# Second layer of the mix MLP by Strassen's seven products instead of eight, with GpSimd adds over SBUF and graph loads on SyncE

## The chip, the cores and the metric

The kernel runs on one core of one Trainium2 chip. The metric is the device time of one execution in microseconds (us). The kernel before takes 1915.63 us, the median of three runs (1912.76 to 1917.06).

## What is computed

One layer of a graph transformer over 1250 tokens of 768 features, all in float32, in three parts:

```
xn = layernorm(x)
x  = x + gnn(xn, edges) + mix(xn)         # mix: linear attention, then an MLP
x  = x + ffn(layernorm(x))                # router picks 2 of 4 experts

mix's MLP:  x = x + gelu(h @ fc1_w + fc1_b) @ fc2_w + fc2_b    # 768 -> 3072 -> 768
gnn:        two graph attention layers (4 heads of 192, 2 heads of 96):
            w[s,d] = exp(leaky(a[s] + b[d]) - max) where an edge is; out[d] = sum_s w[s,d] h[s] / sum_s w[s,d]
```

The change touches the second matrix product of mix's MLP (fc2) and the way in which the graph part, which runs beside that MLP, is cut and loaded.

## The kernel before

Tokens lie in 10 tiles of 125 (`TP`). Big matrix products with 768 inputs already use the seven-product scheme of Strassen and Winograd: both operands are cut in two along both sides, some sums of quarters are formed first (`differences` on the token side, L101; `combined` on the weight side, L111), and seven products of quarters take the place of eight. `product` (L123) issues the matmuls of one product; with `more=True` it goes on adding into a bank of PSUM that already holds an earlier product, so that one bank gathers a chain of sums.

The stage in question begins at L953, where the PSUM pools are dealt anew: two banks for the graph part and transposes (`p_tp`), one for a chained bank of fc1 (`p_a`), two for its other products (`p_dc`) and three for all else (`p_m3`). The hidden 3072 features are taken in 12 groups of 256 (`GROUPS`). Each group has two token units (`MIX`, 250 and 375 token pairs). For each unit `fc1_unit` (L967) makes the hidden values in seven steps, chained, with ScalarE copying the chained bank aside between its products (L982, L992, L995) and VectorE adding (L985, L998, L1005), and the gelus on ScalarE (L965). Then fc2 is applied plainly: `fc2_half` (L1009) makes one tile's half of 384 output columns by two matmuls (the two blocks of 128 hidden features, L1016) and VectorE adds the bank into the running sum `xn` in SBUF (L1021). That is 12 groups x 10 tiles x 2 halves = 240 such halves, 480 matmuls; the hardware issues each float32 matmul as two instructions, so the profile counts 960.

The graph part is a generator (`gnn`, L1177). It first finds the largest score of each target (`largest`, L1058: VectorE passes of 1250 columns, L1086, with the adjacency loaded chunk by chunk over GpSimd's queue, L1067). Then, for three groups of target tiles (`SPLITS`: 4, 3 and 3 tiles), for each head and each of ten source chunks, `weighted` (L1128) makes the edge weights: two exponentials on ScalarE (L1144, L1147), a maximum and a minimum-times-adjacency on VectorE (L1149, L1150); the PE multiplies them with the features (L1194 in layer one, L1233 in layer two). The adjacency, the row `bt` and the features come over GpSimd's DMA queue (L1142, L1133, L1182).

What runs when: a pattern of letters (L1338) deals the seven steps of `fc1_unit` (P) and the halves of the unit before (h) in turn, and each puts PE time on an account (`spend`, L1305). When the account covers the next yield of `gnn`, the graph part moves one step on. A scheduler may then move instructions within each engine's stream; those wrapped in `pin` keep their order. [...] In the last group the tiles are finished one by one (`last_tile`, L1314), so that the expert part can begin.

Of the kernel before, what the change touches and what calls it, by code (L numbers as in the profile page):

```python
# [23 lines left out]
MIX, MIX_TILES = [(0, 250), (250, 375)], [(0, 1, 5, 6), (2, 3, 4, 7, 8, 9)]  # L24
# [8 lines left out]
def tile_gps_layer(ctx, tc, a, out):  # L33
# [77 lines left out]
    def combined(engine, w11, w12, w21, w22, to):  # L111

        s1, s2, s4 = (to[:, i] for i in range(3))
        engine.tensor_tensor(s1, w21, w22, ALU.add)
        engine.tensor_tensor(s2, s1, w11, ALU.subtract)
        engine.tensor_tensor(w21, w11, w21, ALU.subtract)
        engine.tensor_tensor(s4, w12, s2, ALU.subtract)
        return w11, w12, w21, w22, s1, s2, s4
# [35 lines left out]
    at = 0  # L154
# [666 lines left out]
    def load_fc2(g, j):  # L821

        if g < GROUPS:
            c0, w = HALVES[j]
            lasts[g, j] = wpool.tile([128, 2, 384], F32, name="w2", bufs=3)
            nc.sync.dma_start(
                lasts[g, j], rows(fc2[g * 256 : (g + 1) * 256, c0 : c0 + w], 128)
            )
# [5 lines left out]
    with tc.tile_pool(name="qp", bufs=1) as qp:  # L834
        wp = weights(qp, "wp", a["L0_mix_proj_w"])
        load_fc1(0)
        load_fc2(0, 0)
        load_fc2(0, 1)
        load_fc1(1)
        load_fc2(1, 0)  # L840
# [114 lines left out]
    p_dc = banks.enter_context(tc.tile_pool(name="p_dc", bufs=2, space=PSUM))  # L955
    p_mm[0] = banks.enter_context(tc.tile_pool(name="p_m3", bufs=3, space=PSUM))
# [10 lines left out]
    def fc1_unit(g, c):  # L967


        c0, w = MIX[c]  # L970
        cs = slice(c0, c0 + w)
        va, vb = (v_of[c][:, i] for i in range(2))
        x11, x21 = fT[:, 0:3, cs], fT[:, 3:6, cs]
        x22, t3 = fT[:, 3:6, HALF + c0 : HALF + c0 + w], x12[:, :, cs]
        t1, t2, t4 = (xt[:, i, :, cs] for i in range(3))
        w11, w12 = list(quarters_of(firsts[g]))[:2] if c == 0 and g else firsts[g][:2]
        pa = p_a.tile([128, 512], F32, name="ps_a")[:, :w]
        pd, pc = (p_dc.tile([128, 512], F32, name=n, tag="dc")[:, :w] for n in ("ps_d", "ps_c"))
        c1 = u3 = hpool.tile([128, 375], F32, name="c1")[:, :w]
        u2 = hpool.tile([128, 375], F32, name="u2")[:, :w]  # L980
        product(nc.tensor, pa, w11, x11)
        nc.scalar.copy(c1, pa)  # L982
        yield
        product(nc.tensor, pd, w12, x21)
        nc.vector.tensor_tensor(va[:, 0, :], pd, c1, ALU.add)  # L985
        gelu(va[:, 0, :], va[:, 0, :], 2 * g)
        if c == 0 and g:
            fc1_sums(g)
        yield
        _, _, s3, w22, s1, s2, s4 = firsts[g]  # L990
        product(nc.tensor, pa, s2, t2, more=True)
        nc.scalar.copy(u2, pa)  # L992
        yield
        product(nc.tensor, pa, s3, t3, more=True)
        nc.scalar.copy(u3, pa)  # L995
        yield
        product(nc.tensor, pc, s1, t1)
        nc.vector.tensor_tensor(vb[:, 1, :], pc, u3, ALU.add)  # L998
        gelu(vb[:, 1, :], vb[:, 1, :], 2 * g + 1)
        yield  # L1000
        product(nc.tensor, pa, w22, t4, more=True)
        gelu(vb[:, 0, :], pa, 2 * g + 1)
        yield
        product(nc.tensor, pc, s4, x22, more=True)
        nc.vector.tensor_tensor(va[:, 1, :], pc, u2, ALU.add)  # L1005
        gelu(va[:, 1, :], va[:, 1, :], 2 * g)
        yield

    def fc2_half(g, c, t, j):  # L1009

        h, i = divmod(t, 5)
        at = i * TP - MIX[c][0]
        o0, ow = HALVES[j]
        ps = bank("ps_f2")[:TP, :ow]
        for f in range(2):
            nc.tensor.matmul(  # L1016
                ps, v_of[c][:, f, h, at : at + TP], lasts[g, j][:, f, :],
                start=f == 0, stop=f == 1,
            )
        o = xn[:, t, o0 : o0 + ow]  # L1020
        nc.vector.tensor_tensor(o, ps, o, ALU.add)  # L1021
# [4 lines left out]
    av2 = gp.tile([TP, 2, 192], F32, name="av2")  # L1026
    nc.sync.dma_start(av2[:, 0, :], bcast(a["L0_gnn_a_src2"].rearrange("h c -> (h c)"), TP))
    nc.sync.dma_start(av2[:, 1, :], bcast(a["L0_gnn_a_dst2"].rearrange("h c -> (h c)"), TP))
# [5 lines left out]
    def load_wu2x():  # L1034
        nc.vector.memset(wu2x[96:97], 0.0)
        nc.vector.memset(wu2x[:, :, 768:769], 0.0)
        nc.vector.memset(wu2x[96:97, :, 768:769], 1.0)

        nc.gpsimd.dma_start(wu2x[96:97, 0, :768], brow_d)
        nc.gpsimd.dma_start(wu2x[:96, :, :768], rows(a["L0_gnn_Wu"][D : D + 192, :], 96))  # L1040

    h2 = gp.tile([TP, NT, 2, 97], F32, name="h2")
    nc.vector.memset(h2[:, :, :, 96:97], 1.0)
# [14 lines left out]
    def largest(heads, s, b_d, pace, before=lambda c: None, behind=lambda: None):  # L1058
# [3 lines left out]
        load = [slot_x[:TP, 5000 + i * N : 5000 + (i + 1) * N] for i in range(2)]  # L1062
        load.append(turns[:TP, 0, :N])
# [31 lines left out]
        for h in range(heads):  # L1095
            for u0 in range(0, NT, 4):
                n = min(4, NT - u0)
                ps = bank("ps_mx").rearrange("p (u c) -> p u c", c=128)
                for u in range(n):
                    pin(nc.tensor.transpose(  # L1100
                        ps[:TP, u, :TP], run[:, h, (u0 + u) * TP : (u0 + u + 1) * TP],
                        ident[:TP, :TP],
                    ))
                nc.vector.tensor_reduce(
                    mx[:, h, u0 : u0 + n], ps[:TP, :n, :TP], AX.X, ALU.max
                )
            yield 2.0
        sd = s[:, 1]
# [10 lines left out]
        ps = bank("ps_row")  # L1119
# [6 lines left out]
        yield from rest(4)  # L1126

    def weighted(g, h, heads, b_d, s, sl):  # L1128

        t0, n = SPLITS[g]  # L1130
        d0, w = t0 * TP, n * TP
        bt = gp.tile([128, 2, 500], F32, name="bt", bufs=2)
        nc.gpsimd.dma_start(  # L1133
            bt[:, :, :w],
            bcast(
                b_d.rearrange("(j h t) p -> j h (t p)", j=2, h=heads)[:, h, d0 : d0 + w], 128
            ),
        )
        for c in range(NT):
            adj = slot_x[:TP, c * 500 : c * 500 + w]  # L1140
            if h == 0:
                nc.gpsimd.dma_start(adj, adj_d[c * TP : (c + 1) * TP, d0 : d0 + w])  # L1142
            e = gp.tile([TP, 2, 500], F32, name="ee", bufs=2)
# [4 lines left out]
            wt = gp.tile([TP, 500], F32, name="wt", bufs=3)  # L1148
            nc.vector.tensor_tensor(wt[:, :w], e[:, 0, :w], e[:, 1, :w], ALU.max)  # L1149
            nc.vector.scalar_tensor_tensor(  # L1150
                wt[:, :w], wt[:, :w], 1.0, adj, op0=ALU.min, op1=ALU.mult
            )
            yield c, wt[:, :w]

    def lagging(steps, run, lag=1):
        held = []
        for x in steps:
# [3 lines left out]
            yield 1.7  # L1161
# [3 lines left out]
    def earlier():  # L1165


        at = [slot_x[:TP, 5000 + i * D : 5000 + (i + 1) * D] for i in range(3)]
        for t in range(NT + 2):
            if t < NT:  # L1170
                nc.gpsimd.dma_start(at[t % 3], raw_d[t])
            if t > 1:
                o = xn[:, t - 2, :]
                nc.vector.tensor_tensor(o, o, at[(t - 2) % 3], ALU.add)
            yield

    def gnn():  # L1177
        feats = {}

        def fetch(h):  # L1180
            gh = turns[:TP, h % 2, :].rearrange("p (t f) -> p t f", f=193)
            pin(nc.gpsimd.dma_start(gh, rows(g1_d[h % 4], TP)))  # L1182
            feats[h % 4] = gh

        yield from largest(4, s1, b1_d, 5.0, merged, lambda: fetch(0))
        fetch(1)
        for g, (t0, n) in enumerate(SPLITS):
            for h in range(4):
                gh = feats[h]
                sums = [bank4("ps_o").rearrange("p a b -> p (a b)") for _ in range(2)]  # L1190
# [10 lines left out]
                yield from lagging(weighted(g, h, 4, b1_d, s1, s1l), add)  # L1201
                if g < 2 or h < 2:
                    fetch(h + 2)
                for i in range(n):
# [9 lines left out]
                    if h == 3:  # L1214
                        for j in range(2):
                            pr = gp.tile([TP, 2, 96], F32, name="pr")
# [9 lines left out]
        for g, (t0, n) in enumerate(SPLITS):  # L1226
            o2 = turns[:97, 1, :1000].rearrange("p (h n) -> p h n", n=500)
            w = n * TP
            for h in range(2):
# [9 lines left out]
                yield from lagging(weighted(g, h, 2, b2_d, s2, s2l), add)  # L1239
                nc.scalar.copy(o2[:, h, :w], sums[:97, :w])  # L1240
            for i in range(n):
                for h in range(2):
                    rd = small.tile([TP, 1], F32, name="rd")
                    for c0, cw in ((384, 385), (0, 384)):
                        ps = bank("ps_u2")
# [74 lines left out]
    def halves_of(g, c):  # L1320
        ts = MIX_TILES[c]
        if g < GROUPS - 1:
            return [(g, c, t, j) for j in range(2) for t in ts]
        return [(g, c, t, j) for t in ts for j in range(2)]

    def put_half(g, c, t, j):
        fc2_half(g, c, t, j)
        spend(1.39)
        if g == GROUPS - 1 and j:
            last_tile(t)  # L1330

    todo = []
    for g in range(GROUPS):
        if g:
            load_fc1(g + 1)
            load_fc2(g, 1)
            load_fc2(g + 1, 0)
        for c, pattern in enumerate(("PPhhhhPhhPPhhPPhhhh", "PPhhPhhPPhhPPhh")):  # L1338
            if g == GROUPS - 1 and c:
# [3 lines left out]
                gnn_pool.__exit__(None, None, None)  # L1343
            parts = fc1_unit(g, c)
            for p in pattern:
                if p == "P":
                    next(parts)
                    if g or c:
                        spend(2.04 if c else 1.36)
                elif todo:  # L1350
                    put_half(*todo.pop(0))
            todo = halves_of(g, c)
    for x in todo:
        put_half(*x)
# [445 lines left out]
```

## Time and profile before

| what | value |
| --- | --- |
| median of three runs | 1915.63 us |
| the profiled execution's own time | 1917.79 us |
| its span, first to last instruction | 1915.7 us |
| PE busy over the span | 1872.7 us, 98% |
| VectorE (DVE), ScalarE (ACT), GpSimd (POOL) busy | 1355.5, 802.8, 502.7 us |
| the MLP stage with the graph part | 552 to 1355 us of the span |
| fc2's matmul instructions (L1016) | 960, from 558 to 1349 us |

A busy time is the union of an engine's instructions; a matmul's end is modelled and reaches over the start of the next, so the mean duration of a matmul is longer than the distance at which they follow each other. In the groups of instructions each row has the source line, the engine, the operation, what it writes and reads, the shape, the count, the busy time, the mean duration in ns, and the idle time of the engine just before. "PEld" is the load of a matmul's stationary operand, which lies beside the matmuls.

### The profile page before, as it was taken

To read this page: it belongs to the slowest core of one execution; us is meant where nothing else is said; L and a number is where in the kernel's file an instruction comes from. 1 tells how busy PE (TensorE), PEld (TensorE's weight loads), DVE (VectorE), ACT (ScalarE), POOL (GpSimd) and SP (SyncE) were. 2 spreads that over 40 slices of the span, in tenths; PEclk is the share of its full clock that TensorE was granted. 3 is DMA by queue.
4 is the path that set the end of the run, shared out by engine and by line. 5 is a ranking of instruction groups with operands and counts; after the bars stand their busy time and mean duration, and the time that the engine had idled before them with its cause. 6 is when DMAs were issued, how large, how long until landed. Compare 5 with 4: busy or idle time off the path is not lost.

```text
span 1915.7 us, 19523 instructions
## 1 busy us (share of the span) xinstructions
PE 1872.7 (98%) x6966; PEld 1244.2 (65%) x6966; DVE 1355.5 (71%) x2372; ACT 802.8 (42%) x1206; POOL 502.7 (26%) x341
## 2 busy tenths in 40 slices
PE   8999899999999999999999999999999999999998
PEld 7555456775556667787877655566766666666664
DVE  4889651379545986676766977865787777777778
ACT  3223231232321117777775166754473343533330
POOL 2167588777851110020210111100131000000000
PEclk9999999999999999999999999999999999999999
DMA  9957711423149742242432542301485201011023
GB/s 342 274 133 177 200 1 2 116 18 66 2 34 158 142 111 76 70 118 74 113 100 56 149 121 82 92 9 52 130 95 90 76 1 66 1 66 38 20 85 110
DMA packets 184284, 175.49 MB, mean 92 GB/s; under 512 B 110043, under 2 KB 153595, under 8 KB 182908
## 3 DMA queue, kind: packets, MB, share of 16 engines
q0 software_dynamic: 126640, 68.01, 20.7%
q1 hardware_dynamic: 54270, 98.48, 16.3%
q10 hardware_dynamic: 3278, 7.75, 1.3%
q8 instruction: 55, 0.90, 0.2%
q14 instruction: 41, 0.34, 0.1%
HBM read 137.80 MB, written 42.05 MB: 94 GB/s over the span
## 4 chain that ended last, share of the span: by engine, by line
PE 87%; DMA 5%; DVE 3%; issue 2%; ACT 1%; SPq 1%; POOL 0%; DVEq 0%; POOLq 0%; ACTq 0%
PE ps_f L1016 15%; PE ps_p L81 13%; PE ps_r L81 12%; PE ps_a L127 8%; PE ps_o L1194 7%; PE ps_p L913 4%; PE ps_c L127 4%; PE ps_g L536 3%; PE ps_f L1594 3%; PE ps_o L1233 2%; PE ps_va L127 2%; PE ps_qa L127 2%; PE ps_ka L127 2%; PE ps_d L127 2%; PE ps_u L1246 1%
## 5 line engine op out<-in xcount | busy, mean ns | idle before, releaser
L309 POOL DMA_INDIRECT tab<-mult,place_e x170 | 355.7, 2092 | 149.5 <-DMA tab<-mult,place_e 99.0
L1016 PE MATMUL ps_f<-w,v 128*125 128x384 f32 x960 | 337.5, 486 | 0.0
L1016 PEld LDWEIGHTS ps_f<-w,v 128*125 128x125 f32 x960 | 177.7, 188 | 106.0 <-issue 7.5
L1021 DVE TENSOR_TENSOR slot_a<-ps_f,slot_a 125x384 f32<-125x384 f32 x240 | 131.5, 552 | 66.5 <-PE ps_f L1016 62.6
L1149 DVE TENSOR_TENSOR wt<-ee 125x375 f32<-125x375 f32 (+1 forms) x180 | 105.8, 589 | 85.8 <-PE ps_o L1194 57.5
L1194 PEld LDWEIGHTS ps_o<-turns,wt 125*125 125x125 f32 x800 | 136.9, 188 | 29.7 <-DVE wt L1150 4.5
L1194 PE MATMUL ps_o<-turns,wt 125*125 125x193 f32 x800 | 151.6, 329 | 3.5 <-DVE wt L1150 3.5
L1144 ACT ACTIVATE ee<-bt,s 125x375 f32<-125x375 f32 (+1 forms) x180 | 114.8, 638 | 78.0 <-DVE wt L1149 69.5
L81 PE MATMUL ps_p<-fT,w 128*128 128x312 f32 (+1 forms) x432 | 125.5, 426 | 2.1 <-DMA w<-in_L_ffn_w_dram 1.5
L1150 DVE SCALAR_TENSOR_TENSOR wt<-wt,slot_x 125x375 f32<-125x375 f32 (+1 forms) x180 | 105.9, 589 | 4.4
L81 PEld LDWEIGHTS ps_p<-fT,w 128*128 128x128 f32 x432 | 81.5, 189 | 37.9 <-issue 1.7
L81 PE MATMUL ps_r<-w,slot_a 128*125 128x384 f32 x260 | 94.5, 486 | 0.0
L536 PE MATMUL ps_g<-fx,zT 128*125 128x388 f32 x240 | 83.6, 507 | 5.7 <-DVE zT L338 5.2
L127 PE MATMUL ps_a<-fT,w 128*128 128x250 f32 (+1 forms) x288 | 85.4, 426 | 0.7 <-DVE slot_a L918 0.7
L1556 DVE SCALAR_TENSOR_TENSOR slot_x<-ps_r,gate,slot_x 125x384 f32<-125x384 f32 x100 | 60.7, 615 | 33.3 <-PE ps_r L81 33.0
L81 PE MATMUL ps_p<-xt,ws 128*128 128x313 f32 (+1 forms) x288 | 83.6, 425 | 0.0
L503 PE MATMUL ps_u<-wu,fT 128*125 128x384 f32 x240 | 80.0, 490 | 2.4 <-ACT fT L499 2.4
L913 PE MATMUL ps_p<-wp,slot_x 128*125 128x384 f32 x240 | 79.5, 486 | 0.0
L1086 DVE SCALAR_TENSOR_TENSOR slot_x<-turns,s,slot_x 125x1250 f32<-125x1250 f32 x54 | 79.4, 1509 | 0.1
L1147 ACT ACTIVATE ee<-bt,s1l 125x375 f32<-125x375 f32 (+1 forms) x120 | 75.4, 628 | 0.1
L965 ACT ACTIVATE v<-v,par 128x250 f32<-128x250 f32 (+1 forms) x72 | 40.0, 556 | 78.1 <-DVE v L985 31.7
L81 PE MATMUL ps_r<-w2s,ht 128*125 128x384 f32 x200 | 72.7, 486 | 0.0
(403 smaller groups left out, 3432.1 us busy)
## 6 DMA issues: line engine op xcount, KB each, us to landing
turns<-g_d POOLq DMA_DIRECT2D x12, 942.4 KB
w<-in_L_mix_fc_w_dram SPq DMA_DIRECT2D x12, 768.0 KB
w<-in_L_mix_fc_w_dram SPq DMA_DIRECT2D x24, 384.0 KB
slot_x<-tab POOLq DMA_DIRECT2D x14, 610.4 KB
w<-in_L_ffn_w_dram SPq DMA_DIRECT2D x11, 768.0 KB
w<-in_L_ffn_w_dram SPq DMA_DIRECT2D x5, 1536.0 KB
slot_x<-tab POOLq DMA_DIRECT2D x40, 183.1 KB
kr<-key_d SPq DMA_DIRECT2D x6, 1062.5 KB
```

The lines of the kernel that those rows point to most:

```text
L81: return lambda *args, **kw: pin(getattr(self.engine, name)(*args, **kw))
L127: engine.matmul(ps, wt[:, k, :], x[:, k, :], start=k == 0 and not more, stop=k == n - 1, skip_group_check=more,)
L309: nc.gpsimd.indirect_dma_start(out=tabs[c % 2][:, :], out_offset=bass.IndirectOffsetOnAxis(ap=place[:, c : c + 1], axis=0), in_=mult[:, c ...
L503: nc.tensor.matmul(ps[:TP, :w], fT[:, k, tc_], wu[:, k, c0 : c0 + w], start=k == 0, stop=k == KC - 1,)
L536: nc.tensor.matmul(ps[:TP, :388], zT[:, k, :], fx[:, k, h2 * 388 : (h2 + 1) * 388], start=k == 0, stop=k == KC - 1,)
L913: nc.tensor.matmul(ps[:TP, :w], qT[:, k, t * TP : (t + 1) * TP], pm[:, k, c0 : c0 + w], start=k == 0, stop=k == KC - 1,)
L1016: nc.tensor.matmul(ps, v_of[c][:, f, h, at : at + TP], lasts[g, j][:, f, :], start=f == 0, stop=f == 1,)
L1021: nc.vector.tensor_tensor(o, ps, o, ALU.add)
L1144: nc.scalar.activation(e[:, 0, :w], bt[:TP, 0, :w], AF.Exp, bias=s[:, 0, h, c : c + 1])
L1149: nc.vector.tensor_tensor(wt[:, :w], e[:, 0, :w], e[:, 1, :w], ALU.max)
L1150: nc.vector.scalar_tensor_tensor(wt[:, :w], wt[:, :w], 1.0, adj, op0=ALU.min, op1=ALU.mult)
L1194: nc.tensor.matmul(sums[i // 2][:TP, (i % 2) * 193 : (i % 2 + 1) * 193], wt[:, i * TP : (i + 1) * TP], gh[:, c, :], start=c == 0 and i % 2 ...
```

## The change

- fc2 goes over to the seven products: for each group and each pair of tiles (t, t+5) `Pair.run` issues A1, A2, A3 and A4 chained in one bank, D alone, and C1 and C2 chained in another. Each is a single matmul of 384 columns. A1, A2 and A3 are read by a ScalarE copy into SBUF, and GpSimd adds the copy to the running sums (for A1 behind D's add); D, C1, A4 and C2 are read and added by VectorE straight from PSUM. Tiles 4 and 9 of the last unit of the last group stay plain (`direct`).
- The token-side differences of the hidden values are four VectorE subtractions per unit (`second_tokens`), the weight-side sums four GpSimd operations per group (`fc2_sums`).
- PSUM is dealt anew: `p_dc` gets one bank instead of two, the new `p_fd` two, the pool for all else two instead of three; small graph users move to `p_tp`.
- The graph's target groups are 3, 3, 2 and 2 tiles (`DESTS`) in place of 4, 3 and 3. Adjacency, `bt`, features, `raw_d` and `wu2x` loads go over SyncE's queue; the adjacency of the next group is asked for chunk by chunk while the last head of this one still runs.
- Two gelus are issued later within `fc1_unit`; the paces of the graph's yields are set anew.

```diff
-MIX, MIX_TILES = [(0, 250), (250, 375)], [(0, 1, 5, 6), (2, 3, 4, 7, 8, 9)]
+MIX, MIX_TILES = [(0, 250), (250, 375)], [(0, 1), (2, 3, 4)]
+DESTS, DW = [(0, 3), (3, 3), (6, 2), (8, 2)], 375
...
+    def fc2_sums(g, to, apart=None):
+        w = lasts[g]
+        lasts[g] = combined(
+            nc.gpsimd, *(w[:, f : f + 1, c : c + 384] for c in (0, 384) for f in (0, 1)), to,
+            apart,
+        )
...
-    p_dc = banks.enter_context(tc.tile_pool(name="p_dc", bufs=2, space=PSUM))
-    p_mm[0] = banks.enter_context(tc.tile_pool(name="p_m3", bufs=3, space=PSUM))
+    p_dc = banks.enter_context(tc.tile_pool(name="p_dc", bufs=1, space=PSUM))
+    p_fd = banks.enter_context(tc.tile_pool(name="p_fd", bufs=2, space=PSUM))
+    p_mm[0] = banks.enter_context(tc.tile_pool(name="p_m2", bufs=2, space=PSUM))
...
-    def fc2_half(g, c, t, j):
+    def second_tokens(c, w):
+
+        v = v_of[c]
+        of = (v[:, 0:1, 0, :], v[:, 0:1, 1, :], v[:, 1:2, 0, :], v[:, 1:2, 1, :])
+        differences(nc.vector, of, vt, 0, w)
+
+    class Pair:
...
+        def run(self, step):
+            x11, x21, x22, t3, t1, t2, t4 = self.x
+            w11, w12, s3, w22, s1, s2, s4 = lasts[self.g]
+            y1, y2 = xn[:, self.t], xn[:, self.t + 5]
+            if step == "A1":
+                self.pa = bank("ps_fa")[:TP, :384]
+            if step in ("D", "C1"):
+                self.pd = p_fd.tile([128, 512], F32, name="ps_fd", tag="fd")[:TP, :384]
+            x, w, o, more = {
+                "A1": (x11, w11, y1[:, :384], False), "D": (x21, w12, y1[:, :384], False),
+                "A2": (t2, s2, y2[:, :384], True), "C1": (t1, s1, y2[:, 384:], False),
+                "A3": (t3, s3, y2[:, 384:], True), "A4": (t4, w22, y1[:, 384:], True),
+                "C2": (x22, s4, y2[:, :384], True),
+            }[step]
+            ps = self.pa if step[0] == "A" else self.pd
+            product(nc.tensor, ps, x, w, more=more)
+            if step in ("A1", "A2", "A3"):
+
+                c = hpool.tile([TP, 384], F32, name="part", bufs=3)
+                nc.scalar.copy(c, ps)
+                if step == "A1":
+                    self.c1 = c
+                else:
+                    pin(nc.gpsimd.tensor_tensor(o, o, c, ALU.add))
+            else:
+                nc.vector.tensor_tensor(o, ps, o, ALU.add)
+            if step == "D":
+                pin(nc.gpsimd.tensor_tensor(o, o, self.c1, ALU.add))
+
+    ORDERS = (
+        "A1p Dp A1q C1p A2p Dq A3p A2q A4p C2p A3q C1q A4q C2q",
+        "A1p Dp A1q C1p Dq A2p A3p A2q C2p A4p A3q C1q A1r A4q C2q A2r Dr C1r A3r C2r A4r",
+        "A1p Dp A1q C1p A2p Dq A2q C2p A3p C1q A3q A4p C2q A4q",
+    )
...
+    def load_adj(g, c):
+
+        if g < len(DESTS):
+            d0, w = DESTS[g][0] * TP, DESTS[g][1] * TP
+            by_parts(nc.sync, adj_of[:, c, :w], adj_d[c * TP : (c + 1) * TP, d0 : d0 + w])
...
-            if h == 0:
-                nc.gpsimd.dma_start(adj, adj_d[c * TP : (c + 1) * TP, d0 : d0 + w])
-            e = gp.tile([TP, 2, 500], F32, name="ee", bufs=2)
+            e = gp.tile([TP, 2, DW], F32, name="ee", bufs=2)
...
+            if h == heads - 1:
+                load_adj(g + 1, c)
             yield c, wt[:, :w]
...
-            yield 1.7
+            yield pace
...
-            pin(nc.gpsimd.dma_start(gh, rows(g1_d[h % 4], TP)))
+            by_parts(nc.sync, gh, rows(g1_d[h % 4], TP))
             feats[h % 4] = gh
 
-        yield from largest(4, s1, b1_d, 5.0, merged, lambda: fetch(0))
+        yield from largest(4, s1, b1_d, 5.6, merged, lambda: fetch(0))
...
-        for c, pattern in enumerate(("PPhhhhPhhPPhhPPhhhh", "PPhhPhhPPhhPPhh")):
+        last = g == GROUPS - 1
+        for c, pattern in enumerate(("PpppPpppPpppPpppPpppPpppPpp", "PpXpPppPppPppPppPppPpp")):
...
+                elif p == "X":
+                    while todo:
+                        put(todo.pop(0))
+                    if last:
+                        vt = late.tile([128, 3, 1, 375], F32, name="vt_l")
+                    second_tokens(0, 250)
+                    load_fc2(g + 1)
...
+                        fc2_sums(g, sums_x)
+                    todo = products_of(g, 0)
```

## The prediction

> **What bounds the kernel now.** I read the busy rows of the page first, then the chain of work that ended last in order of time, then the busy time by stretches of the MLP stage, and last the groups of instructions there. In the chain, fc2 (L1016) is the largest item:
>
> ```profile
> PE ps_f L1016 15%; PE ps_p L81 13%; PE ps_r L81 12%; PE ps_a L127 8%; PE ps_o L1194 7%; PE ps_p L913 4%; PE ps_c L127 4%; PE ps_g L536 3%; PE ps_f L1594 3%; PE ps_o L1233 2%; PE ps_va L127 2%; PE ps_qa L127 2%; PE ps_ka L127 2%; PE ps_d L127 2%; PE ps_u L1246 1%
> ```
>
> In order of time it stands there in lines like this one (start, us, what), and gives the real price of a matmul: 2.58 / 8 = 0.3225 us per instruction, not the 486 ns of its row, whose end is modelled.
>
> ```profile
> 567.39 2.58 PE ps_f L1016 x8
> ```
>
> I cut the stage where VectorE adds the second step of a group's first unit (L985): groups 1-3 are mostly `largest`, 4-7 the first graph layer's weights, 8-10 `largest` and weights of the second layer. The last two lines are group 2 and group 8 alone. Columns: stretch, length, then PE, PEld, DVE, ACT, POOL busy, clock, DMA share, GB/s.
>
> ```profile
> 585.30:744.50 159.20, 155.73 (x563) 103.21 (x562) 119.28 (x167) 37.23 (x61) 22.47 (x26) 0.99 0.62 127
> 744.50:1063.50 319.00, 319.00 (x1432) 249.65 (x1431) 225.50 (x477) 227.12 (x339) 44.61 (x51) 1.00 0.33 90
> 1063.50:1269.00 205.50, 204.16 (x679) 122.00 (x678) 167.33 (x298) 125.85 (x195) 26.39 (x47) 1.00 0.34 92
> 1269.00:1355.00 86.00, 85.66 (x362) 57.65 (x360) 50.07 (x140) 35.04 (x60) 0.00 (x0) 1.00 0.16 50
> 632.00:680.00 48.00, 48.00 (x166) 30.94 (x165) 47.71 (x58) 7.00 (x15) 5.65 (x7) 1.00 0.69 129
> 1063.50:1112.80 49.30, 49.30 (x183) 32.38 (x182) 46.65 (x71) 6.89 (x14) 8.32 (x16) 1.00 0.58 147
> ```
>
> The reader is to see two things. The PE is the bound through the whole stage, idle for 5 us of 803. And VectorE has no room in `largest`: 47.71 of 48.00 us. The rows that price the new work:
>
> ```profile
> L1021 DVE TENSOR_TENSOR slot_a<-ps_f,slot_a 125x384 f32<-125x384 f32 x240 | 131.5, 552 | 66.5 <-PE ps_f L1016 62.6
> L1149 DVE TENSOR_TENSOR wt<-ee 125x375 f32<-125x375 f32 x120 | 65.5, 546 | 53.2 <-PE ps_o L1194 39.0 <-PE ps_o L1233 7.1 <-ACT ee L1147 5.3
> L1144 ACT ACTIVATE ee<-bt,s 125x375 f32<-125x375 f32 x120 | 72.4, 604 | 53.7 <-DVE wt L1149 53.3
> L995 ACT COPY c<-ps_a 128x375 f32<-128x375 f32 x12 | 5.6, 468 | 29.0 <-PE ps_a L127 28.6
> L1005 DVE TENSOR_TENSOR v<-ps_c,u 128x250 f32<-128x250 f32 x12 | 5.0, 414 | 7.8 <-PE ps_c L127 7.6
> L194 POOL MEMSET pattern<- 128x1250 f32 x1 | 1.1, 1143 | 0.0
> ```
>
> **PE.** Before: 480 matmuls. After: 12 groups x 5 pairs x 7 = 420, less 7 and plus 8 for the pair done plainly: 421. 59 matmuls x 2 x 0.3225 = 38.1 us off. The graph's matmuls keep their columns; layer two has 20 more matmuls for four groups (250 columns where 500 were), which by columns cost nothing and by start-up at most 0.5 us. PE: -37.5 us, all of it on the path, about 3.2 us per group of 48.
>
> **VectorE.** fc2's adds stay 240 (four of seven products, plus four plain ones). New are the token differences, per group 4 x 0.414 + 4 x 0.546 = 3.8 us, 46 in all, and 120 more weight operations of the same total columns: rows of 375 and 500 columns are 546 and 675 ns, so 0.16 us is fixed, 120 x 0.16 = 19 us. I added up the changed program's order on VectorE by these rows, less 0.045 us per instruction because they overlap (476 instructions of groups 4-7 add up to 244 us by duration and are busy for 225.5). Groups 1-3: 128 us against a PE need of 143; groups 4-7: 243 against 312; groups 8-10: 179 against 191. Within these, group 2 asks 51 us where the PE asks 45, group 8 asks 54 to 49: there VectorE becomes the bound.
>
> **ScalarE.** 177 copies of 384 columns at the 0.468 us of the copy row, 83 us, and 120 more exponentials, whose rows of 375 and 500 columns (604 and 706 ns) leave 0.3 us fixed: 36 us. Table loads are 91 after, 95 before, for gelu and exponentials together. Groups 4-7: 286 us against 312 of the PE, 91%; before 227 of 319. The copies sit on the path now: the bank of A1 to A4 can take the next product only when its copy is done, and the copy stands behind exponentials and gelus that are queued on ScalarE. In between the order places two to four other products, 1.3 to 2.6 us, which hide a copy of 0.47 us and one or two exponentials, not a table load (1.28 us) on top of these.
>
> **GpSimd.** It loses most of its DMA issues (some 75 of the 107 us it was busy with in the stage) and gets 177 adds and 48 weight sums. The trace has no two-input GpSimd operation. The nearest row is the memset, one stream, 1143 ns for 1250 columns: 0.35 us for 384 columns. The Trainium skill, "GPSIMD Engine Reference", section 3.1, has an add of 2048 float32 at 4497 ns; per column that makes an estimate of 0.85 us, 0.9 with a start. Between 0.4 and 0.9 I take 0.9, since the memset reads nothing: 15 adds and 4 sums, 17 us per group of 45. GpSimd itself has room; the sums s1 and s2 of the next group stand behind the adds of the last pair and must be there for C1 and A2, some 7 us of products later, against about 5 us of copy, add and two sums. It holds unless GpSimd is kept waiting.
>
> Here a rule speaks against the change. The memory page "SBUF — State Buffer", section "Who interferes with whom", says that a VectorE instruction with two SBUF inputs and a GpSimd instruction that reads SBUF exclude each other for a whole instruction. No row here shows it: GpSimd only issued DMAs, beside which L1149 stays at 0.54 us. About 0.6 of VectorE's time in the stage is of that kind (L1086, L1149, L1150, the differences and sums); the PSUM adds are not. By the rows the loss is zero; by the rule at most the whole 0.9 us for each of the 225 operations, 200 us. Taking the 0.6 as the chance to meet, and half of an operation as the wait, gives 0.27 us each, 5 us per group. VectorE then needs 143, 263 and 194 us in the three stretches, where the PE needs 143, 312 and 191.
>
> **DMA and waits.** Loads on SyncE's queue stand in order before the fc1 and fc2 weights: the longest wait of such a load before is 29 us (`bt` for ScalarE), and weights are asked for one group, 45 us and more, ahead, so they stay hidden; with that cover gone it would be a fetch of a few us in a group. The PE's idle of 3.5 us in groups 1-3, at the row that goes to DRAM and back as `bt`, shrinks, since the adjacency is asked for earlier and two more yields lie before: -2 us, between -3.5 and 0. The differences stand between the last gelus of a unit and C1; 5.7 to 8 us of PE work lie there against 4 to 5 us of add, table load, gelus and one subtraction: hidden on most units.
>
> **The sum.** The profiled execution took 1917.8 us; the median of runs is 2 us lower. 1917.8 - 37.5 - 2 = 1878.3 would be the PE's own pace. Where one engine passes the PE, group by group with the 5 us: group 2 asks 56 to 45 (+11), group 8 60 to 49 (+11), group 9 61 to 59 (+2), together +24, of which neighbours with slack (group 1 has 3 us, group 10 nine) take perhaps a third: +16. Chained banks behind ScalarE at 91% in groups 4-7: four groups at 1 us, +4. 1878.3 + 20 = 1898 as profiled, 1896 in the median of runs; I say 1897.
>
> **Rivals.** (1) The PE's pace, nothing else late: 1878 as profiled, 1877 in the runs. For it: group 2 before has VectorE at 99% without a PE wait. Against it: there the halves had three free banks, now chained ones. With a few us of waits 1884. Chance 0.15. (2) Slower: GpSimd's reads hold the shared port for whole instructions in front of VectorE. At a loss of 0.9 us per operation VectorE needs 128 + 57 x 0.9 = 179, 243 + 68 = 311 and 179 + 51 = 230 us: 36 + 0 + 39 us over the PE, 1878 + 75 = 1953. It decides from a loss of 0.6 us on: with 114 operations in the two stretches and 27 us of slack, 114 x 0.6 - 27 = 41 us eats the gain. For it: the rule, and that VectorE is the fullest engine where its operations have two SBUF inputs. Against it: GpSimd also waits for VectorE, and adds from PSUM run beside it. Chance 0.33, typically near 1935. (3) The chained banks: ScalarE's lag reaches the PE at each of 177 copies by 0.2 us, 35 us, no change: 1915. Chance 0.1: half of it within 0.2%, the rest to both sides.
>
> **How the numbers follow.** The likeliest case, a part of the gain left, has 0.42, with its own range of 1887 to 1910. Faster is this, rival 1 and 0.03 of rival 3: 0.6. Within 0.2% (4 us, what a measurement of this kernel can tell from no change): 0.05. Slower: rival 2 and 0.02 of rival 3, 0.35. The range from 1882 to 1943 leaves out the bare PE pace and the worst of rival 2.
>
> **What would show it.** fc2's matmuls 842 instructions at 0.32 us; groups of about 45 us where only fc2 and fc1 run; GpSimd adds near 0.9 us. Right in its middle: PE waits in groups 2 and 8 for VectorE's reads of the D and C banks, and few elsewhere. Rival 2: L1161, L1238 and L1239 clearly longer in the mean than 1509 and 546 ns, the PE waiting on VectorE in all stretches. Rival 3: the PE waiting for the `part` copies. I would be wrong from the ground if GpSimd's adds take several us, since then the three `part` buffers hold ScalarE and with it the PE.

## The result and the profile after

The changed kernel takes 1972.29 us, the median of four runs (1970.86 to 1974.66), against 1914.45 us of the kernel before on the same chip: a ratio of 1.030 (95% interval 1.028 to 1.032). It is slower by 58 us; the forecast was 1897. The profiled execution took 1970.9 us with a span of 1969.1.

The page's busy rows and the head of its chain, of the kernel after:

```profile
PE 1866.9 (95%) x6888; PEld 1225.6 (62%) x6888; DVE 1472.3 (75%) x2588; ACT 894.0 (45%) x1501; POOL 711.6 (36%) x464
...
PE 66%; DVE 16%; issue 6%; DMA 5%; ACT 4%; POOL 2%; ACTq 0%; SPq 0%; DVEq 0%; POOLq 0%
```

Before, the PE held 87% of that chain and VectorE 3%. Now VectorE holds 16%: the end of the kernel goes through VectorE far more often. The same cuts of the stage as before the change, at VectorE's add of the second step of a group's first unit (columns: stretch, length, then PE, PEld, DVE, ACT, POOL busy, clock, DMA share, GB/s). The first three lines are groups 1-3, 4-7 and 8-10, the last three groups 1, 2 and 8:

```profile
585.00:766.10 181.10, 149.05 (x505) 90.03 (x504) 142.09 (x183) 40.87 (x87) 106.57 (x77) 0.95 0.68 120
766.10:1092.90 326.80, 315.98 (x1419) 244.30 (x1418) 267.99 (x594) 276.41 (x494) 88.85 (x80) 1.00 0.40 97
1092.90:1320.00 227.10, 206.58 (x675) 120.29 (x674) 201.93 (x349) 138.05 (x252) 79.02 (x64) 0.98 0.34 94
...
585.00:652.80 67.80, 49.91 (x161) 30.89 (x159) 37.47 (x52) 14.02 (x30) 33.65 (x29) 0.87 0.82 125
652.80:713.70 60.90, 50.98 (x158) 28.05 (x158) 59.59 (x63) 14.05 (x30) 45.15 (x29) 1.00 0.75 119
1092.90:1155.10 62.20, 53.31 (x174) 31.05 (x173) 61.23 (x77) 13.56 (x29) 33.06 (x25) 0.95 0.44 116
```

The stretches grew from 159.2, 319.0 and 205.5 us to 181.1, 326.8 and 227.1, 51 of the 53 us by which the span grew. Two kinds of loss are to be seen. In groups 2 and 8 VectorE is full (59.59 of 60.90, 61.23 of 62.20), and the PE, once busy all the time, is left idle. In group 1 no engine is full: VectorE has 37.47 of 67.80 us. The granted clock is 0.87 there, because of one long pause of the PE (last section).

The rows that price the new work, from the page's groups of instructions (GpSimd's adds, ScalarE's copies, VectorE's adds from PSUM, the passes of `largest`):

```profile
L1057 POOL TENSOR_TENSOR slot_a<-slot_a,part 125x384 f32<-125x384 f32 x118 | 146.9, 1253 | 216.0 <-ACT part L1053 214.1
L1059 DVE TENSOR_TENSOR slot_a<-ps_fd,slot_a 125x384 f32<-125x384 f32 x177 | 96.6, 549 | 53.8 <-PE ps_fd L130 29.5
L1053 ACT COPY part<-ps_fa 125x384 f32<-125x384 f32 x177 | 83.0, 471 | 109.6 <-PE ps_fa L130 79.6
L1161 DVE SCALAR_TENSOR_TENSOR slot_x<-turns,s,slot_x 125x1250 f32<-125x1250 f32 x54 | 102.5, 1937 | 0.1
```

and from the groups with shapes kept apart, the two weight operations of 375 columns:

```profile
L1239 DVE SCALAR_TENSOR_TENSOR wt<-wt,slot_x 125x375 f32<-125x375 f32 x120 | 79.4, 667 | 2.2
L1238 DVE TENSOR_TENSOR wt<-ee 125x375 f32<-125x375 f32 x120 | 77.1, 647 | 31.4 <-ACT ee L1236 18.3 <-PE ps_o L1290 12.0 <-ACT part L1053 0.5
```

VectorE's operations with two SBUF inputs are longer: the passes at L1161 1937 ns in the mean where the same ones took 1509, the weight operations 647 and 667 where they took 546. Its add from PSUM, with one SBUF input, stayed: 549 ns, 552 before. Single instructions make it plain. L1161 takes 1.51 us in the ten that no GpSimd operation overlaps, 2.04 in the mean of the 44 that one does. In a stretch of the timeline in group 2 (start, us, engine, line, what, and the idle time before):

```profile
656.96 3.68 DVE L1161 SCALAR_TENSOR_TENSOR slot_x<-turns,s,slot_x 125x1250 f32<-125x1250 f32 x2
657.18 2.14 POOL L1061 TENSOR_TENSOR slot_a<-slot_a,part 125x384 f32<-125x384 f32 x1 [1.24 <-DVE slot_a L1059]
659.29 2.21 POOL L1057 TENSOR_TENSOR slot_a<-slot_a,part 125x384 f32<-125x384 f32 x1
```

Two passes of 3.0 us take 3.68, and the two GpSimd adds, 1.00 us each where nothing is in their way, take 2.14 and 2.21. The times fit two engines that stand aside for whole operations of each other: the first pass alone would end at 658.47 us, and 1.00 us after that is 659.47, where the first add ends at 659.32.

Group 1 is another matter. The timeline of the kernel after, GpSimd first, then VectorE and the PE:

```profile
593.76 4.61 POOL L1125 DMA_DIRECT2D tab<-tab  x3
604.89 0.57 POOL L1142 DMA_DIRECT2D bts<-tab  x1 [6.52 <-DMA tab<-tab]
611.58 0.54 POOL L1142 DMA_DIRECT2D h<-tab  x1 [6.12 <-DMA tab<-tab]
612.13 1.01 POOL L1057 TENSOR_TENSOR slot_a<-slot_a,part 125x384 f32<-125x384 f32 x1
...
613.17 0.56 DVE L1059 TENSOR_TENSOR slot_a<-ps_fd,slot_a 125x384 f32<-125x384 f32 x1 [10.12 <-POOL slot_a L1057]
619.45 0.95 DVE L1157 TENSOR_SCALAR turns<-bts 125x1250 f32<-125x1250 f32 x1 [5.72 <-DMA bts<-tab]
...
606.68 0.81 PE L130 MATMUL ps_fd<-w,v 128*125 128x384 f32 x2
623.96 1.64 PE L130 MATMUL ps_fa<-w,v 128*125 128x384 f32 x2 [16.47 <-DVE slot_a L1059]
```

and GpSimd's timeline of the kernel before:

```profile
560.55 4.64 POOL L1054 DMA_DIRECT2D tab<-tab  x3 [2.14 <-DMA tab<-mult,place_e]
571.32 0.57 POOL L1067 DMA_DIRECT2D slot_x<-tab  x1 [6.14 <-DVE slot_a L1021]
```

The three DMAs that merge the parts of the adjacency (L1125 now, L1054 before) stand in GpSimd's pinned stream behind group 0's adds, so they start at 593.8 us instead of 560.6. Each chunk load (L1142) then waits over 6 us for such a merge, at the head of GpSimd's queue. An add (L1057) is queued behind, a VectorE add to the same running sum waits 10.1 us for it, VectorE then waits 5.7 us for the chunk itself, and the PE stands for 16.5 us.

### The profile page after: what moved, and what is told of

The parts are those of the page before. It is cut to its first block, busy times and chain, and to the rows that moved or that the text cites. A ratio compares the mean times of both kernels' runs of the same rounds, so it can differ in the third digit from the quotient of the medians.

```text
span 1969.1 us, 20576 instructions
## 1 busy us (share of the span) xinstructions
PE 1866.9 (95%) x6888; PEld 1225.6 (62%) x6888; DVE 1472.3 (75%) x2588; ACT 894.0 (45%) x1501; POOL 711.6 (36%) x464
## 4 chain that ended last, share of the span: by engine, by line
PE 66%; DVE 16%; issue 6%; DMA 5%; ACT 4%; POOL 2%; ACTq 0%; SPq 0%; DVEq 0%; POOLq 0%
PE ps_p L82 13%; PE ps_r L82 11%; PE ps_o L1290 5%; PE ps_a L130 4%; PE ps_p L918 4%; PE ps_fa L130 4%; DVE slot_x L1161 3%; PE ps_fd L130 3%; PE ps_f L1714 3%; PE ps_c L130 2%; PE ps_va L130 2%; DVE slot_a L1059 2%; PE ps_qa L130 2%; PE ps_ka L130 2%; DVE wt L1238 2%
## 5 line engine op out<-in xcount | busy, mean ns | idle before, releaser
L1057 POOL TENSOR_TENSOR slot_a<-slot_a,part 125x384 f32<-125x384 f32 x118 | 146.9, 1253 | 216.0 <-ACT part L1053 214.1
L1061 POOL TENSOR_TENSOR slot_a<-slot_a,part 125x384 f32<-125x384 f32 x59 | 81.0, 1373 | 253.3 <-DVE slot_a L1059 230.9
L1238 DVE TENSOR_TENSOR wt<-ee 125x375 f32<-125x375 f32 (+1 forms) x240 | 136.0, 572 | 48.1 <-ACT ee L1236 30.1
L1290 PE MATMUL ps_o<-turns,wt 125*125 125x193 f32 x800 | 155.0, 329 | 10.1 <-DVE wt L1239 7.5
L1233 ACT ACTIVATE ee<-bts,s 125x375 f32<-125x375 f32 (+1 forms) x240 | 132.4, 552 | 47.6 <-DVE wt L1238 46.8
L1239 DVE SCALAR_TENSOR_TENSOR wt<-wt,slot_x 125x375 f32<-125x375 f32 (+1 forms) x240 | 136.6, 575 | 4.5
L1059 DVE TENSOR_TENSOR slot_a<-ps_fd,slot_a 125x384 f32<-125x384 f32 x177 | 96.6, 549 | 53.8 <-PE ps_fd L130 29.5
L1053 ACT COPY part<-ps_fa 125x384 f32<-125x384 f32 x177 | 83.0, 471 | 109.6 <-PE ps_fa L130 79.6
L130 PE MATMUL ps_fa<-w,v 128*125 128x384 f32 x228 | 95.9, 502 | 24.5 <-DVE slot_a L1059 22.1
L1161 DVE SCALAR_TENSOR_TENSOR slot_x<-turns,s,slot_x 125x1250 f32<-125x1250 f32 x54 | 102.5, 1937 | 0.1
L1236 ACT ACTIVATE ee<-bts,s1l 125x375 f32<-125x375 f32 (+1 forms) x160 | 87.5, 547 | 0.1
```

The costliest lines, as they stand in the source:

```text
L130: engine.matmul(ps, wt[:, k, :], x[:, k, :], start=k == 0 and not more, stop=k == n - 1, skip_group_check=more,)
L1057: pin(nc.gpsimd.tensor_tensor(o, o, c, ALU.add))
L1161: pin(nc.vector.scalar_tensor_tensor(run[:, h, :], far, sc, run[:, h, :], op0=ALU.min, op1=ALU.max))
L1233: nc.scalar.activation(e[:, 0, :w], bt[:TP, 0, :w], AF.Exp, bias=s[:, 0, h, c : c + 1])
L1236: nc.scalar.activation(e[:, 1, :w], bt[:TP, 1, :w], AF.Exp, bias=sl[:, h, c : c + 1])
L1239: nc.vector.scalar_tensor_tensor(wt[:, :w], wt[:, :w], 1.0, adj_of[:, c, :w], op0=ALU.min, op1=ALU.mult)
```

## The experiments

The theory from these lines: two costs, both of GpSimd's 177 adds. One is the port, the lengthening of both engines' operations; the other is the order of GpSimd's queue, with DMAs that wait in it ahead of adds and adds ahead of DMAs. The rivals: the chain of dependence, in which VectorE waits for GpSimd at the running sums; ScalarE's copies and the chained banks; and the graph part's new groups and loads. Ratios are against the kernel before on the same chip.

**e1, the adds left out.**

```diff
-                    pin(nc.gpsimd.tensor_tensor(o, o, c, ALU.add))
+                    pass
...
-            if step == "D":
-                pin(nc.gpsimd.tensor_tensor(o, o, self.c1, ALU.add))
```

> GpSimd's 177 adds are left out (two thirds of the A products are copied and never reach the running sums); the copies, the weight sums on GpSimd and all else stay. PE need alone is about 1880 us as profiled. Theory 1 (shared SBUF port: VectorE's operations with two SBUF inputs are held by GpSimd's adds) and theory 2 (GpSimd's in-order queue makes VectorE and ScalarE wait for adds) together: 1890 to 1905 us. Theory 3 (the chained banks behind ScalarE's copies lose the time by themselves): stays over 1940. Theory 4 (the graph's new cutting and its loads on SyncE lose it): stays over 1940.

Measured 1904.71 us, 0.993 (0.992 to 0.995). So the adds cost 68 us, more than the whole loss, and the chained banks and copies, which are still there, are not the cause. What is left is 13 us faster than before (0.0067 of 1917), where the PE's part alone was put at 37.5.

**e2, the same adds on a tile of their own.**

```diff
+    aside = hpool.tile([TP, 384], F32, name="aside")
+    nc.gpsimd.memset(aside, 0.0)
...
-                    pin(nc.gpsimd.tensor_tensor(o, o, c, ALU.add))
+                    pin(nc.gpsimd.tensor_tensor(aside, aside, c, ALU.add))
...
-                pin(nc.gpsimd.tensor_tensor(o, o, self.c1, ALU.add))
+                pin(nc.gpsimd.tensor_tensor(aside, aside, self.c1, ALU.add))
```

> GpSimd makes its 177 adds on a tile of its own and not on the running sums, so no VectorE add waits for a GpSimd add, while GpSimd reads and writes SBUF as before (the running sums lack these terms). Theory 1 (port): most of the loss stays, 1950 to 1965 us, and VectorE's 1250-column pass stays near 1.9 us. Theory 2 (VectorE waits for GpSimd's adds): falls by 30 us or more, to 1940 or less.

Measured 1976.35 us, 1.030 (1.028 to 1.032): above both ranges, and nothing is gained. The dependence between the engines at the running sums costs nothing that the total shows, although the waits of after name it. VectorE's timeline shows why in group 1:

```profile
624.49 4.86 DVE L1160 TENSOR_SCALAR turns<-bts 125x1250 f32<-125x1250 f32 x1 [18.26 <-DMA bts<-tab]
```

Freed of the 10.1 us for the add, VectorE waits 18.3 us for the chunk, and the PE behind it 20.8: both waits had the one cause, the late merge.

**e3, the chunk loads over SyncE's queue.**

```diff
-                pin(nc.gpsimd.dma_start(load[c % 3], adj_d[c * TP : (c + 1) * TP, :]))
+                by_parts(nc.sync, load[c % 3], adj_d[c * TP : (c + 1) * TP, :])
```

> The chunk loads of the pass for the largest scores go over SyncE's queue in place of GpSimd's; the adds no longer stand behind loads that wait for the merging DMAs. Theory 2 (queue order): the 18 us of PE idle in group 1 and a part of group 8's 9 us go, 1945 to 1955 us. Theory 1 (port): the loss is in the lengthened operations, at most 5 us less, 1967 to 1972.

Measured 1967.44 us, 1.026 (1.025 to 1.028), 5 to 7 us better. The merges are still late (they start at 595.4 us), and so are the chunks, on whatever queue they come. So this run doesn't tell the two theories apart.

**e4, the graph part alone.** fc2 plain as before, with the PSUM pools and patterns of before; the graph's groups, loads and paces as after.

```diff
-        for c, pattern in enumerate(("PpppPpppPpppPpppPpppPpppPpp", "PpXpPppPppPppPppPppPpp")):
+        for c, pattern in enumerate(("PPhhhhPhhPPhhPPhhhh", "PPhhPhhPPhhPPhh")):
...
-                    put(todo.pop(0))
+                    put_half(*todo.pop(0))
```

> Only the graph part of the change: four target groups, loads over SyncE, small graph users in the other PSUM pool; fc2 is plain with eight half products and the PSUM pools, patterns and tiles of before. Theory 4 (the new cutting costs): 1930 us or more. Theories 1 to 3 (the fc2 part costs): 1910 to 1922, about as before.

Measured 1909.04 us, 0.995 (0.993 to 0.997): the graph part by itself gains 8 us in this run (e10, with the same graph part, gains 3). The waits of its PE in the stage come to 0.2 us; the cost is all in fc2's half of the change.

**e5, all seven products added by VectorE from PSUM**, no copies, no GpSimd adds.

```diff
-            if step in ("A1", "A2", "A3"):
...
-            else:
-                nc.vector.tensor_tensor(o, ps, o, ALU.add)
-            if step == "D":
-                pin(nc.gpsimd.tensor_tensor(o, o, self.c1, ALU.add))
+            nc.vector.tensor_tensor(o, ps, o, ALU.add)
```

> VectorE reads and adds all seven products from PSUM itself; no copies on ScalarE, no adds on GpSimd (its weight sums stay). VectorE gets 177 x 0.5 = 88 us more of work with one SBUF input, which GpSimd does not hold up, ScalarE loses 83 us. Needs of VectorE by the rows against the PE: groups 1-3 157 to 143, 4-7 273 to 312, 8-10 207 to 191 us. Theory 1 and 2 (GpSimd's adds are the cause): 1880 + 14 + 16 and some waits, 1905 to 1925 us. Theory 3 (the chained banks as such): 1950 or more, since a chained bank now waits for a VectorE fuller than before.

Measured 1921.74 us, 1.002 (1.001 to 1.003). With 177 adds of 0.55 us more, 97 us, put on VectorE, the kernel is 51 us faster than with the adds on GpSimd. The edit takes away the port's cost, the queue's and ScalarE's copies at once; the next two separate the first two.

**e6, GpSimd as busy, but only writing.** In place of each add three memsets of the copy.

```diff
-                    pin(nc.gpsimd.tensor_tensor(o, o, c, ALU.add))
+                    for _ in range(3):
+                        pin(nc.gpsimd.memset(c, 0.0))
...
-                pin(nc.gpsimd.tensor_tensor(o, o, self.c1, ALU.add))
+                for _ in range(3):
+                    pin(nc.gpsimd.memset(self.c1, 0.0))
```

> Each of GpSimd's 177 adds is replaced by three memsets on the copy (together about 1.07 us, waiting for the copy and holding its buffer as the add does, in the same place of GpSimd's order), which write SBUF and read none; the running sums lack these terms. Theory 1 (the shared read port): VectorE's operations go back to 1.51 and 0.55 us and 30 us or more go, to 1920 to 1945. Theory 2 (GpSimd's order: merging DMAs and copies behind adds): stays at 1965 to 1976, with the wait for the first adjacency chunk still there.

Measured 1927.17 us, 1.005 (1.003 to 1.006). Its groups of instructions:

```profile
L1163 DVE SCALAR_TENSOR_TENSOR slot_x<-turns,s,slot_x 125x1250 f32<-125x1250 f32 x54 | 81.8, 1557 | 0.1
...
L1058 POOL MEMSET part<- 125x384 f32 x354 | 149.1, 424 | 333.9 <-ACT part L1053 320.8
```

Three memsets are 1.27 us, as long as an add, in the same place of the queue and behind the same copies, and VectorE's passes are back at 1557 ns. What is left over 1509 comes from GpSimd's 48 weight sums, which read SBUF and stay in every run with seven products: by overlap in this trace, the 31 passes with only memsets beside them take 1509 ns in the mean (longest 1521), the 7 with a weight sum beside them 1872. Against e2, which also leaves VectorE without a wait for GpSimd's sums, 0.025 of 1916 us, 49 us, are the price of the adds' reading: the port. Group 1 still takes 67.4 us, since the queue's order is unchanged.

**e7, the merges ahead of the adds.** The first three merges right after group 0's weight sums, chunk loads on SyncE.

```diff
-        for c in range(3):
-            before(c)
...
                         fc2_sums(g, sums_x)
+                    if g == 0:
+                        for i in range(3):
+                            merged(i)
```

> The change as it is, with the first three merging DMAs put ahead of group 0's adds in GpSimd's order and the chunk loads on SyncE, so that the first chunk of adjacency is not late. Theory 2: group 1 goes back from 68 to about 50 us and the total to about 1950. Theory 1: at most 5 us less than with the chunk loads on SyncE alone (1967).

Measured 1953.68 us, 1.019 (1.018 to 1.021), 19 us better than after, of which the loads on SyncE alone (e3) gave 5 to 7. GpSimd's timeline:

```profile
564.64 4.59 POOL L1125 DMA_DIRECT2D tab<-tab  x3
```

The merges start 29 us earlier, and group 1 falls from 67.8 to 51.0 us.

**e8, e5 with the mask pass of `largest` on ScalarE**, to see whether e5's rest is VectorE's load.

```diff
-            pin(nc.vector.tensor_scalar(far, adj, -2.0 * NEG, NEG, op0=ALU.mult, op1=ALU.add))
+            pin(nc.scalar.activation(far, adj, AF.Identity, bias=low, scale=-2.0 * NEG))
```

> As with all adds on VectorE, and the 20 preparing passes over an adjacency chunk (0.80 us each on VectorE) done by ScalarE, which is idle in those stretches: 16 us less for VectorE where it is the bound. If VectorE's load in groups 1-3 and 8-10 is what is left (theory 1 without GpSimd), 8 to 14 us less than all adds on VectorE; if the chained banks wait by themselves, no change.

Measured 1908.26 us, 0.995 (0.994 to 0.996), 13 us better than e5, and in the groups with `largest`: groups 2 and 8 fall from 59.4 and 60.6 us to 55.0 and 54.4.

**e9, e8 with the graph's paces spread out**, so that `largest` takes longer and the weights run closer together.

```diff
-        yield from largest(4, s1, b1_d, 5.6, merged, lambda: fetch(0))
+        yield from largest(4, s1, b1_d, 6.6, merged, lambda: fetch(0))
...
-                yield from lagging(weighted(g, h, 4, b1_d, s1, s1l), add, 0.49 * n)
+                yield from lagging(weighted(g, h, 4, b1_d, s1, s1l), add, 0.45 * n)
...
-        yield from largest(2, s2, b2_d, 4.5)
+        yield from largest(2, s2, b2_d, 5.4)
```

> All adds on VectorE, preparing passes on ScalarE, and the pass for the largest scores spread wider (a step per 6.6 and 5.4 us of PE time in place of 5.6 and 4.5), the weights closer (0.45 in place of 0.49 per tile). If what is left is VectorE's load in groups 2, 3 and 8 (48 to 49 of 50 us there, 80 to 90% elsewhere): group 2 falls from 55 towards 48 and the total to 1895 to 1905. If the chained banks wait by themselves: no change, 1906 to 1912.

Measured 1900.19 us, 0.992 (0.990 to 0.993): faster than both kernels, with the whole computation. Its three stretches:

```profile
587.20:735.00 147.80, 142.18 (x490) 89.32 (x489) 136.04 (x206) 33.12 (x52) 27.70 (x25) 0.99 0.54 106
735.00:1052.40 317.40, 314.16 (x1437) 247.29 (x1436) 275.52 (x668) 249.64 (x431) 19.74 (x20) 1.00 0.43 105
1052.40:1250.60 198.20, 192.80 (x656) 117.15 (x655) 183.93 (x362) 122.04 (x203) 19.06 (x18) 0.99 0.40 109
```

They are 5, 5 and 7 us over the PE's need of 143, 312 and 191 us, now that VectorE is relieved in the groups where it was full. Group 2 went from 55.0 to 52.5 us only.

**e10, e4 with the mask pass on ScalarE**: the same edit where the PE is the bound.

> The graph part of the change alone with plain fc2 (1909 us), and the preparing passes on ScalarE. There the PE is busy all through, so relief for VectorE should bring nothing: 1907 to 1911. It is the measure for whether seven products with VectorE's adds win anything over eight.

Measured 1912.37 us, 0.998 (0.998 to 0.999), no better than e4. So e8 gains because VectorE is late there, not because the pass is cheaper on ScalarE. It also sets seven products against eight with the same graph part and the same passes: 0.995 (e8) against 0.998, some 7 us of the 37.5. Eight products with the paces of e9 were not tried.

**e11, e9 with the paces further out** (7.4, 0.42 and 6.2).

> The same with 7.4 and 6.2 us and 0.42. VectorE's load as the cause: a further few us, or a loss in the weights' groups when ScalarE and VectorE fill up there; 1890 to 1910.

Measured 1903.00 us, 0.993 (0.991 to 0.994): groups 1-3 (142.9 us) and 8-10 (194.0) gain 9 us on e9, groups 4-7 (322.7) give back 5, and what follows group 10 gives back 8. The paces of e9 are about right.

**e12, e7 and e6 together**: merges first, and GpSimd only writing.

> Both suspected costs taken away at once: the adds replaced by memsets of the same waits and about the same time (write-only, the running sums lack these terms), the first merging DMAs ahead of them and the chunk loads on SyncE. If the shared port (1976 to 1927) and GpSimd's order (1972 to 1954) are all that the adds cost, it comes to the time without any adds, 1904 to 1911 us. If something third is left of the adds, such as ScalarE waiting for GpSimd to free a copy, it stays at 1915 or more.

Measured 1901.36 us, 0.992 (0.990 to 0.994), beside e1's 1904.71: without the adds' reads and with the queue's order mended, nothing is left of the adds' 68 us. The three stretches, first of e7, with the port's cost and without the queue's, then of e12, with neither:

```profile
588.50:753.50 165.00, 147.44 (x505) 89.70 (x504) 144.69 (x184) 40.61 (x87) 94.50 (x64) 0.99 0.58 119
753.50:1079.20 325.70, 315.52 (x1418) 244.27 (x1417) 267.46 (x595) 276.24 (x494) 86.04 (x76) 1.00 0.41 97
1079.20:1303.10 223.90, 204.24 (x675) 119.64 (x674) 199.02 (x348) 137.72 (x252) 81.50 (x58) 0.98 0.34 95
...
585.80:732.10 146.30, 142.73 (x504) 89.72 (x503) 127.23 (x182) 40.46 (x87) 83.73 (x155) 1.00 0.61 128
732.10:1049.30 317.20, 313.50 (x1419) 245.31 (x1418) 248.38 (x593) 275.08 (x494) 91.21 (x198) 1.00 0.41 100
1049.30:1257.30 208.00, 200.41 (x675) 120.80 (x674) 183.69 (x348) 135.94 (x252) 74.19 (x148) 0.98 0.36 103
```

VectorE is busy 52 us less in e12, and the stretches are 43 us shorter, in groups 4-7 too, where VectorE was far from full. The PE's largest waits in them (what, on whom, us in total, times, longest), in e7:

```profile
PE ps_o L1326 <- DVE wt L1237: 11.2, 15, 2.6
PE ps_o L1288 <- DVE wt L1237: 7.5, 8, 1.3
PE ps_fd L130 <- DVE slot_a L1059: 6.5, 6, 2.2
PE ps_fa L130 <- DVE slot_a L1059: 6.2, 7, 2.0
```

and in e12:

```profile
PE ps_o L1328 <- DVE wt L1239: 2.8, 4, 1.5
PE ps_fa L130 <- DVE slot_a L1060: 2.6, 3, 1.8
PE ps_o L1290 <- DVE wt L1239: 2.5, 4, 0.9
PE ps_fd L130 <- DVE slot_a L1060: 1.9, 1, 1.9
```

The port's waits are many and short, 31 us in these lines of e7 against 10 in e12: for the graph's weights (18.7 us against 5.3) and for reads of the product banks (12.7 against 4.5). With the smaller lines, the PE is idle for 47 us in e7 and 15 in e12, 41 and 12 of them on VectorE. The other 11 of the 43 us lie in the PE's busy time, whose ends are modelled; what they are stays open.

## Why the prediction was wrong

The side was wrong, and the case that came was rival 2, the shared port, together with a cost that no case had. The signs that it named for this rival came: L1161, L1238 and L1239 at 1937, 647 and 667 ns against 1509 and 546, and the PE waiting on VectorE in all stretches.

**The failed step** is what the sum made of GpSimd's adds: the way from "0.27 us each, 5 us per group" of VectorE's time to "+16" of path. Two things are to be kept apart.

- *VectorE's load was sized nearly right, in part by luck.* The 0.27 was a chance times half an operation, not a measurement. In after VectorE lost 86 us over the 225 GpSimd operations (its operations beside one, against the same ones alone), 0.38 us each. For the adds alone, e7 against e12, it is 52 us in ten groups, 5.2 a group. VectorE's busy time by stretch, predicted as 143, 263 and 194 us, were 142, 268 and 202 in the windows of after. And GpSimd's add took 1.00 us alone where the estimate from the Trainium skill's "GPSIMD Engine Reference", section 3.1, was 0.9.
- *What the sum made of it was wrong.* It took each group for the largest of its engines' totals and let neighbours lend their slack, so that the 5 us per group came to 9 us of path: the sum's +16 against the +7 that the same working gives without them (group 2 +6, group 8 +5, a third taken by neighbours). The runs show 49 us (e2 to e6) and 52 (e7 to e12, 0.027 of 1916). By group, e7 against e12: group 2 takes 61.6 us instead of 50.9 and group 8 61.1 instead of 56.2, 16 us in all. The other eight groups from 1 to 10 lose 27 us, where the sum had put +2 (group 9). In groups 4-7 VectorE is busy for 267 of 326 us in e7, so it is not full, and the PE waits for it all the same. A delay of up to 2.4 us (the longest pass took 3.87 us for 1.51) falls in front of one weight or one bank that the PE needs next. Each pair of tiles has one bank for D and C and one chained bank; whether more banks would let the PE run ahead of the delays was not tried. Nor did the sum count the other side of the lock: the 225 GpSimd operations took 292 us instead of 225, and the copies behind them waited (ScalarE's copy waits 23.0 us for GpSimd in e7, 6.8 in e12).

The rule of the Trainium skill's page "SBUF — State Buffer" ("Who interferes with whom") was therefore the right one to heed, and this case's runs now stand behind it: passes with two SBUF inputs 1937 ns in the mean with GpSimd's adds and 1557 with its memsets, adds from PSUM 549 ns, unmoved. The page's words "for the whole instruction" stand with another mode of VectorE; for two SBUF inputs they fit the timeline of group 2 above. The prediction put 0.33 on it. Its break-even at 0.6 us per operation came from the same totals and was too high: at 0.38 us the gain was already eaten (e7, without the queue's cost, is at 1953.68).

**The missed step** is GpSimd's queue. "It holds unless GpSimd is kept waiting" named the danger, but the adds were not laid beside the DMAs that GpSimd keeps, the merges and the chunk loads of `largest`, though the order of the changed program was there to be read. That cost 19 us with the adds (after to e7) and, in e6 to e12, 0.0128 of 1916 us, 25 us, 19 of them in group 1. That GpSimd loses most of its DMA issues was true of the stage as a whole, not of group 1, where its merges and chunk loads are.

**The other steps.**

- PE -37.5 us: right as a count. The pages list 7006 matmul instructions for e4 and 6888 for e12 and after, 118 fewer, at 0.3225 us each. Little of it became time, since the PE waits more: e12's stretches are 146.3, 317.2 and 208.0 us where the PE needs 143, 312 and 191.
- "DMA and waits", -2 us: too small by e4, which shows -8, with no wait of the PE left but 0.2 us. With e10 at -3 the size stays unsure.
- Groups 2 and 8, VectorE the bound: right in place (59.59 of 60.90 and 61.23 of 62.20 us busy), and without the port nearly right in size: 50.9 and 56.2 us in e12 for the predicted 51 and 54.
- VectorE's overlap was put at 0.045 us per instruction; the figures beside it (244 and 225.5 us, 476 instructions) give 0.039, 3 us more in groups 4-7.
- Rival 3, the chained banks behind ScalarE: wrong. e1 and e12 keep the copies and the banks, and their PE waits for a copy are 1.2 us in e12.

The account: PE -37.5 and the graph's waits -8 would be about 1870. The 1901 to 1905 of e12 and e1 are some 30 us over that. Part of this rest is VectorE's load in the groups with `largest`: e8 and e9 gain 13 and 6 to 8 us by relieving it, in a kernel whose stretches are longer in the same places. That the same would come off e12 was not tried, nor what the 48 weight sums cost, so how the rest divides stays open. On top, the port of the adds is +49 to +52 and the queue's order +19 to +25. The last two come to 68 to 77 us, the adds as a whole to 68 (after to e1).

## What to carry to other kernels

An add moved to an idle engine isn't free if it shares a port with the engine that is nearly full: here 177 SBUF adds on GpSimd cost 68 us, while the same adds as PSUM reads on VectorE, 97 us more for the fuller engine, cost some 17 (e5 beside e1, and e5 has no ScalarE copies either). Totals of an engine per stretch say where it is full, not what a lock of one microsecond in front of the next matmul costs; where the PE runs close behind that engine, count such a delay nearly in full: here 52 us of VectorE's time became 43 us of the three stretches. And before work goes onto a queue that also issues DMAs, lay the queue's order out: each DMA that waits there holds the work behind it, and each pinned operation holds the DMAs.

## What the runs showed of the hardware

The pause in group 1 seems to have cost more than its 16.5 us. Stretches of the kernel after around it (columns as above):

```profile
592.00:612.00 20.00, 15.49 (x55) 9.99 (x53) 5.16 (x12) 3.64 (x8) 6.54 (x6) 0.99 1.06 110
612.00:622.00 10.00, 0.00 (x0) 0.00 (x0) 3.07 (x4) 0.48 (x1) 8.24 (x9) 0.50 1.21 237
622.00:632.00 10.00, 8.04 (x18) 4.67 (x19) 6.50 (x9) 2.04 (x4) 4.24 (x5) 0.66 0.23 61
```

The granted clock is 0.50 in the pause and 0.66 in the 10 us after it, and the first two matmuls then take 1.64 us where the same two took 0.81. The Trainium skill's page "TensorE: Matmul & The Clock Gate", Part 1, tells of this half clock after an idle time; here, as an estimate, the long wait of the PE is paid for by some 2 to 3 us more (8 us of work at a clock of 0.66 where 0.99 was granted before).

Also not expected: GpSimd's add of two 384-column operands takes 1.00 us alone and up to 3.37 beside VectorE, and its memset of 384 columns 0.42 to 0.46 in the mean (e6 and e12), without lengthening VectorE's passes (1509 ns in e6 with only memsets beside them).
